# Cross-attention kernel on one core: weight loads dealt to other slots, other orders at head and end

## The chip, the cores and the metric

The kernel runs on one core of one Trainium2 chip. The metric is the device time of an execution in microseconds; a time is the median over several executions. Profiles come from one further execution, taken with the hardware profiler.

The engines are named as in the profile: PE does matmuls, PEld loads their stationary operand, DVE, ACT and POOL work elementwise, SP issues DMAs. "L694" is line 694 of the kernel.

## The reference

For 8 batches with 256 rows of 1024 values each, and a context of 256 rows per batch:

```
xn     = layernorm(x) * gamma + beta            # per row
Q      = xn @ Wq.T                              # 1024 x 1024, 32 heads of 32
scores = Q_h @ ctx_h.T / sqrt(32), masked       # context is keys and values
attn   = softmax(scores) @ ctx_h
out    = x + attn @ Wout.T
```

All is float32, and the mask is all true in these inputs.

## The kernel before

**Slots.** A slot n stands for batch `n // 8` and a group of four heads `n % 8`; there are N = 64. Loop pass n (L903) issues, for every engine, work of several slots: the scores of slot n+1, the values (probabilities times context) of slot n-2, a part of the query product of a later batch and a part of the output product of the batch before. The order in which each engine gets its instructions is the order in which the Python calls stand (`manual_schedule`, L115): nothing is reordered. SP, too, issues its DMAs in this order, and one that has to wait holds all those behind it.

**Softmax of a slot** (`softmax_parts`, L491). DVE adds the mask and finds the minimum (L515), ACT takes the exponential (L519), DVE inverts the sum (L526), POOL scales (L528), DVE transposes blocks of 32 (L534) into `pT`. A `tail` (L595) ends it: two DMAs pT<-pT (L600), the loads of a list `between`, then two DMAs pT<-pc (L604), which wait until the first two have landed. The loads of a list `ahead` are issued before the tail (L606). In slots 1 to 7 and near the end, the tail itself is put off into the next slot's softmax.

**Two products by Strassen's scheme.** For batches 3 to 7 the query product is done in seven steps, one a slot, from slot n = 8(b-1)+2 on (`firsts`, L782; `query_product`, L432; `Q_PRODUCTS`, L409). Each multiplies a quarter of x, or a sum of quarters, by a quarter of the weights, or a sum of them. Four of the weight operands stay in SBUF. The other three share one tile, `ring` (2 halves of 512 KB): T1 is used in slot n (product S1), B11 in slot n+2 (A11), T3 in slot n+4 (S3). They were written to DRAM once (`keep_wq`) and are loaded anew for every batch (`load_ring`, L405), in the slots that a table gives (L845). A load into a half must wait until the product before it has read that half; the product waits for each half by itself.

The output product of each batch goes the same way, seven products of four steps (`PRODUCTS`, L647; `STEPS`, L654), from 8 slots later on. Its weights `wo` (L162) hold B11, B21, B12 and B22, of which each is loaded by two DMAs of 512 KB (`load_wo`, L169), and four sums T1 to T4 that POOL makes (`sum_wo`, L177). The first batch's steps begin in slot 9: B11 first, then B21. In batch b's first slots the residual rows are loaded (`load_res`, L148); `store` (L734) adds the product to one of them on DVE and sends it out.

**Head** (L851 to L880). The first rows of x are normalised, transposed by PE into a bank, and copied out with gamma and beta in eight chunks `copy_x0` by ACT and DVE; PE takes the chunks in the same order for the first query (`first_q`, L279).

**End** (L1021 on). The last batch's output product is written out by hand. Its sums S2, S1 and S4 are made chunk by chunk (`end_sum`, L748), a chunk for each slot of the last four, and `end_steps` (L758) issues the matmuls; `last` holds the product A11, and four banks collect the rest. Chunk 1 is slot 61, whose values are copied out by ACT at L635.

Of the kernel before, what the change touches and what calls it, by code (L numbers as in the profile page):

```python
# [59 lines left out]
def xattn_kernel(  # L60
# [11 lines left out]
    nc = tc.nc  # L72
# [4 lines left out]
    NQ = NC  # L77
# [9 lines left out]
    N = B * NQ  # L87
# [75 lines left out]
    B11, B21, B22, T1, T2, T3, T4 = range(7)  # L163
    B12 = T1
# [105 lines left out]
    def copy_x0(s, c, engine):  # L270

        to, pt = xnT0[:, c, ts(s, P)], px0[s, c // (NC // 2)][:, c % (NC // 2), :]
        g, b = gam[:, c : c + 1], bet[:, c : c + 1]
        if engine is nc.scalar:
            nc.scalar.activation(to, pt, AF.Identity, bias=b, scale=g)
        else:
            nc.vector.tensor_scalar(to, pt, g, b, ALU.mult, ALU.add)
# [390 lines left out]
    def sum_at(b, name, c=slice(0, NK)):  # L668
        if name == "S2" and c.start == 0:
            s2s[b] = up.tile([P, NK, P], F32, tag="s2", name=f"s2_{b}")  # L670
        one, two, op = {
            "S3": ("A11", "A21", ALU.subtract), "S2": ("A22", "S3", ALU.subtract),
            "S1": ("S2", "A11", ALU.add), "S4": ("A12", "S2", ALU.subtract),
        }[name]
        nc.gpsimd.tensor_tensor(
            operand(b, name)[:, c], operand(b, one)[:, c], operand(b, two)[:, c], op
        )
# [70 lines left out]
    def end_sum(chunks, engine):  # L748
        for name, one, two, op in (
            ("S2", "A22", "S3", ALU.subtract), ("S1", "S2", "A11", ALU.add),  # L750
            ("S4", "A12", "S2", ALU.subtract),
        ):
            engine.tensor_tensor(
                end_operand(name)[:, chunks], end_operand(one)[:, chunks],
                end_operand(two)[:, chunks], op,
            )

    def end_steps(po, name, which, chunks, begins=(), cols=slice(0, 512)):  # L758

        for c in chunks:  # L760
            nc.tensor.matmul(  # L761
                po, end_operand(name)[:, c], wo[:, which, c, cols],
                start=c in begins, stop=True, skip_group_check=True,
            )
# [77 lines left out]
    ):  # L842
        away[n].append(partial(keep_wq, name, half))
    for n, b in firsts.items():
        for slots, name in (((n - 3, n - 2), "T1"), ((n, n), "B11"), ((n + 2, n + 2), "T3")):  # L845
            if b > SPLIT or name != "T1":
                for half, slot in enumerate(slots):
                    rings[slot].append(partial(load_ring, name, half))
# [4 lines left out]
    ln_norm(0, 0, nc.vector)  # L853
    ln_stats(0, 1, (1, 2))
    transpose_x0(0)
    early, late = (0, 1, 2, 3, 6, 7), (4, 5)
    for c in early + late:
        copy_x0(0, c, nc.vector if c > 5 else nc.scalar)
    nc.gpsimd.tensor_copy(xnT0[:, :, S], bet)
    ln_norm(0, 1, nc.vector)  # L860
    first_q(0, early + late)
# [41 lines left out]
    for n in range(N):  # L903
        b, i = divmod(n - NQ, NQ)
        new_q = new_qs[n]
        between = []
        if n % 2 and n + 1 < N:
            between.append(partial(load_v, n + 1))
        elif n % 2 == 0 and n + 4 < N:
            between.append(partial(load_k, n + 4))  # L910
        ahead = rings[n]
        if n + 3 in firsts or n + 2 in firsts:
            between, ahead = between + ahead, []
        if b >= 0:
            if b == B - 2 and i - 1 in (5, 6):
                between.append(partial(send, b, *ENDS_TO[i - 1]))
            if i < 4:
                between.append(partial(load_res, b, *((0, 0), (0, 1), (1, 1), (1, 0))[i]))
        between += [partial(load_x, *args) for args in loads[n]]
        between += [partial(load_mask, one) for one in masks[n]]  # L920
        if n < NQ:
            which, pair = (
                (B12, 0), (B22, 0), (B11, 0), (B12, 1), (B22, 1), (B11, 1), (B21, 0), (B21, 1)
            )[n]
            between.append(partial(load_wo, which, pair))
        if n == N - 4:
            again = xp.tile([P, NS, D], F32, tag="x", name="x_again")
            for s in range(NS):
                between.append(partial(nc.sync.dma_start, again[:, s, :], x[B - 1, ts(s, P), :]))

        if n + 1 < N:
            scores(n + 1)
        project_steps(n, 0)
        hooks, now, behind = {}, [], []
        for what, one, *args in evacuations[n]:
            if one == B - 2:
                now.append(partial(what, one, *args))
            else:
                place = "p1" if what is keep_p1 else "soon" if i == 2 else 0 if i in (3, 4, 6) else 1
                hooks.setdefault(place, []).append(partial(what, one, *args))  # L940
        if n >= 2:
            values(n - 2)
        project_steps(n, 1)
        copies = [partial(copy_q, q) for q in new_q]
        if n in halves and n % 2 == 0:
            make_q(halves[n], second=True, chunks=range(NC // 2, NC))
            copies.insert(0, partial(copy_q, halves[n]))
        for q in new_q:
            make_q(q)
        if n in products:  # L950
            query_product(*products[n])
            copies.append(partial(copy_product, *products[n]))
        for one in now:
            one()
        fill = []
        if n < 2:
            transpose_x1(2 * n)
            transpose_x1(2 * n + 1)
            fill = [partial(copy_x1, 2 * n), partial(copy_x1, 2 * n + 1)]
        elif n <= NQ:  # L960
            fill = [partial(ln_stats, *args, parts=(i,)) for args in stats[n] for i in range(3)]
            fill += [partial(blocks_x, *args) for args in trans[n]]
        if n + 1 < N:
            softmax(n + 1, copies, ahead, between, hooks, fill)
        else:
            copy_at(n - 2)
            for load in between:
                load()
        if b >= 0 and i == 1:
            sum_at(b, "S2", *((slice(NK - 1, NK),) if b == B - 2 else ()))  # L970
        later = []
        if n > NQ:
            for args in stats[n]:
                ln_stats(*args, later=later)
        for args in norms[n]:
            ln_norm(*args, nc.scalar)
        if n > NQ:
            for args in trans[n]:
                blocks_x(*args)
        for args in moves[n]:  # L980
            move_x(*args)
        for one in away[n]:
            one()
        for one in biases[n]:
            mask_bias(one)
        project_steps(n, 2)
        for one, slot in S3_SLOTS:
            if n == slot:
                sum_at(one, "S3")
        if b >= 0:  # L990
            for name in {2: ("S4",), 3 if b == B - 2 else 5: ("S1",)}.get(i, ()):
                sum_at(b, name)
            if i == 0 and b == B - 2:
                sum_at(b, "S2", slice(0, NK - 1))
        for slot, name in ((n + 2, "S1"), (n + 2, "S2"), (n + 1, "S4"), (n - 1, "S3")):
            if slot in firsts:
                sum_x(firsts[slot], name)
        if b == B - 2:
            if i > 2:
                add_kept(b, i, *ENDS_TO[i])  # L1000
        elif b >= 0 and i in (3, 4, 5):
            add_p1(b, *{3: (0, 1), 4: (1, 1), 5: (1, 0)}[i])
        for one in later:
            one()
        if n in halves and n % 2:
            make_q(halves[n], second=True, chunks=range(NC // 2))
        if n == 0:
            nc.gpsimd.tensor_scalar(gs, gam, NEG_SCALE, 1.0, ALU.mult, ALU.mult)
        if n < NQ:
            fold(n)  # L1010
        for one in sums[n]:
            one()
        if N - NQ + 2 < n < N - 1:

            c = n - (N - NQ + 3)
            if c == 0:
                last = ps_q.tile([P, 512], F32, tag="pq", name="po_last")
            end_steps(last, "A11", B11, (c,), (0,))
# [11 lines left out]
        )  # L1030

    nc.scalar.copy(end_p1, last)
    end_sum(slice(0, 2), nc.gpsimd)
    nc.gpsimd.tensor_tensor(r00, r00, end_p1, ALU.add)
    nc.gpsimd.tensor_tensor(r01, r01, end_p1, ALU.add)
    to_c11, to_c21, to_c22, to_c12 = (
        ps_s.tile([P, 512], F32, tag="sc", name=f"po_end_{i}") for i in range(4)
    )
    for c in range(2):
        end_steps(to_c11, "A12", B21, (c,), (0,))  # L1040
        end_steps(to_c21, "A22", T4, (c,), (0,))
    values(N - 2)
    copy_at(N - 2)
    end_sum(slice(2, 3), nc.gpsimd)
# [6 lines left out]
    copy_at(N - 1)  # L1051
    end_sum(slice(3, 4), nc.vector)
    first_cols, last_cols = slice(0, 384), slice(384, 512)
    end_steps(to_c22, "S1", T1, range(2), (0,))
    end_steps(s2t2, "S2", T2, (2,))
    for r in (r01, r10, r11):
        end_add(r, s2t2)
# [61 lines left out]
```

## Time and profile before

| | us |
|---|---|
| median of 3 runs | 575.49 |
| lowest and highest | 574.64, 575.76 |
| the profiled execution's own time | 579.34 |
| its span on the core | 577.6 |

| the profiled execution | us | share of the span |
|---|---|---|
| PE | 567.7 | 98% |
| PEld | 392.2 | 68% |
| DVE | 458.6 | 79% |
| ACT | 412.1 | 71% |
| POOL | 404.7 | 70% |

| stretch of the span, us | PE busy | DMA engines' busy share | GB/s |
|---|---|---|---|
| 0 to 8 | 6.43 | 0.75 | 241 |
| 8 to 150 | 139.16 of 142 | 0.72 | 219 |
| 150 to 240 | 90.00 of 90 | 0.77 | 228 |
| 240 to 250 | 7.81 of 10 | 0.65 | 196 |
| 250 to 545 | 295.00 of 295 | 0.69 | 199 |
| 545 to 578 | 29.31 of 33 | 0.37 | 115 |

The first table sets the profiled execution beside the plain runs. The second gives the time in which each engine worked, as a share of the span. The third cuts the span into stretches: the time in which PE was busy in each, and the mean share of the 16 DMA engines' time that was in use. The ends of matmuls are modelled, so a busy PE isn't PE at its peak; a gap in it is idle time.

### The profile page before, as it was taken

What the parts mean: (1) busy time and instruction counts of PE and PEld (TensorE: products, weight loads), DVE (VectorE), ACT (ScalarE), POOL (GpSimd) and SP (SyncE); (2) the same over time, 40 slices, a digit from 0 to 9 for tenths busy, and PEclk for the clock granted to TensorE, in tenths of its full rate; (3) what the DMA queues carried; (4) which work ended last, traced back from release to release, by engine and by line L of the source; (5) the groups of instructions that cost most, each with busy time, mean ns of one, the idle gap of its engine ahead of it and who ended that gap; (6) DMA issues with size and microseconds to landing.
All of it is one profiled execution on the core that took longest, in us unless ns stands there. A gap on an engine that the chain in (4) does not pass through costs nothing.

```text
span 577.6 us, 20001 instructions
## 1 busy us (share of the span) xinstructions
PE 567.7 (98%) x7162; PEld 392.2 (68%) x7162; DVE 458.6 (79%) x1695; ACT 412.1 (71%) x1425; POOL 404.7 (70%) x672
## 2 busy tenths in 40 slices
PE   8999998999999999899999999999999999999998
PEld 8788884666667777477776677667766777755444
DVE  6897887687878878678888888888877868879823
ACT  4688886677758857678577976779767866869820
POOL 1788998699896896665657775676656667448780
PEclk9999999999999999999999999999999999999999
DMA  8675778756778667776686767887658865436741
GB/s 312 224 211 184 218 240 209 244 172 196 196 229 271 215 188 219 225 222 202 181 247 181 233 196 201 237 257 217 186 160 254 239 192 147 130 112 182 214 154 74
DMA packets 47475, 117.98 MB, mean 204 GB/s; under 512 B 9104, under 2 KB 9872, under 8 KB 47376
## 3 DMA queue, kind: packets, MB, share of 16 engines
q1 hardware_dynamic: 47088, 116.69, 68.2%
q8 instruction: 57, 0.93, 0.7%
q14 instruction: 42, 0.34, 0.2%
q10 hardware_dynamic: 288, 0.01, 0.0%
HBM read 65.28 MB, written 11.53 MB: 133 GB/s over the span
## 4 chain that ended last, share of the span: by engine, by line
PE 79%; POOL 8%; DVE 6%; issue 2%; DMA 2%; ACT 1%; SPq 0%; DVEq 0%; POOLq 0%; ACTq 0%
PE po_S L694 17%; PE pq_A L440 16%; PE sc L479 10%; PE po_A L694 10%; PE pv L622 9%; PE pq_S L440 6%; POOL e L528 6%; PE pq L340 6%; DVE e L515 3%; PE po_end L761 2%; DVE pT L534 1%; PE po_last L761 1%; POOL wo L183 1%; DMA pT<-pT 1%; ACT e L519 1%
## 5 line engine op out<-in xcount | busy, mean ns | idle before, releaser
L528 POOL TENSOR_SCALAR e<-e,rden 128x256 f32<-128x256 f32 x512 | 237.0, 483 | 131.1 <-DVE rden L526 129.6
L519 ACT ACTIVATE e<-e,mn 128x256 f32<-128x256 f32 x512 | 254.0, 500 | 53.8 <-DVE mn L515 53.8
L534 DVE STREAM_TRANSPOSE pT<-e 128x512 f32<-128x512 f32 x256 | 180.7, 707 | 54.8 <-POOL e L528 43.8
L515 DVE CUSTOM_DVE_ANT_0 e<-sc,mb 128x256 f32<-128x256 f32 x512 | 185.9, 416 | 23.7 <-PE sc L479 23.2
L540 ACT COPY pc<-pT 128x512 f32<-128x512 f32 x128 | 79.0, 617 | 72.0 <-DVE pT L534 43.0
L519 ACT ACTIVATION_READ_ACCUMULATOR e<-e,mn 128x1 f32 x512 | 97.7, 191 | 0.0
L340 PE MATMUL pq<-xnT,wq 128*128 128x256 f32 (+1 forms) x368 | 84.1, 383 | 0.0
L340 PEld LDWEIGHTS pq<-xnT,wq 128*128 128x128 f32 x368 | 68.7, 190 | 14.3 <-issue 3.9
L479 PEld LDWEIGHTS sc<-k,qa 32*128 32x128 f32 x1024 | 46.2, 184 | 42.4 <-issue 20.6
L694 PE MATMUL po_S<-wo,at 128*128 128x512 f32 x152 | 74.5, 607 | 0.3 <-DVE r L736 0.3
L622 PE MATMUL pv<-pT,v 64*32 64x128 f32 x4096 | 74.3, 274 | 0.0
L622 PEld LDWEIGHTS pv<-pT,v 64*32 64x32 f32 x4096 | 56.9, 105 | 25.3 <-issue 11.9
L479 PE MATMUL sc<-k,qa 32*128 32x256 f32 x1024 | 73.6, 400 | 0.1
L694 PE MATMUL po_A<-wo,at 128*128 128x512 f32 x128 | 61.9, 616 | 4.2 <-issue 2.2
L694 PE MATMUL po_S<-wo,s 128*128 128x512 f32 x104 | 50.2, 606 | 0.3 <-DVE r L736 0.3
L515 DVE DVE_READ_ACCUMULATOR2_ANT mn<- 128x1 f32 x512 | 42.6, 83 | 0.0
L694 PEld LDWEIGHTS po_A<-wo,at 128*128 128x128 f32 x128 | 22.6, 190 | 29.2 <-issue 23.4
L526 DVE RECIPROCAL rden<-den 128x2 f32<-128x2 f32 x256 | 37.5, 146 | 5.9 <-ACT e L519 4.6
L440 PEld LDWEIGHTS pq_A<-xnT,wq 128*128 128x128 f32 x320 | 37.3, 192 | 4.8 <-issue 4.1
L694 PEld LDWEIGHTS po_S<-wo,at 128*128 128x128 f32 x152 | 25.6, 190 | 20.8 <-issue 19.3
L440 PE MATMUL pq_A<-xnT,wq 128*128 128x128 f32 x320 | 37.3, 275 | 0.0
L635 ACT COPY at<-pv 128x128 f32<-128x128 f32 x128 | 26.2, 253 | 8.7 <-PE pv L622 8.7
(95 smaller groups left out, 605.3 us busy)
## 6 DMA issues: line engine op xcount, KB each, us to landing
v<-in_kv_dram SPq DMA_DIRECT2D x32, 512.0 KB, 4.2
pT<-pT SPq DMA_DIRECT2D x128, 128.0 KB, 2.9
pT<-pc SPq DMA_DIRECT2D x128, 128.0 KB, 4.7
ring<-kept_T SPq DMA_DIRECT2D x18, 512.0 KB, 5.8
k<-in_kv_dram SPq DMA_DIRECT2D x32, 256.0 KB, 3.0
x<-in_x_dram SPq DMA_DIRECT2D x14, 512.0 KB, 5.5
r<-in_x_dram SPq DMA_DIRECT2D x28, 256.0 KB, 4.5
out_dram<-r SPq DMA_DIRECT2D x28, 256.0 KB, 3.9
```

The lines of the kernel that those rows point to most:

```text
L340: nc.tensor.matmul(pqs[n], wq[:, o, c, :], xnTs[b](c), start=(c == 0), stop=(c == NC - 1),)
L440: nc.tensor.matmul(pqs[b][:, o, :], w[:, c], x_[:, c], start=begins and o + c == 0, stop=c == NK - 1, skip_group_check=True,)
L479: nc.tensor.matmul(scs[n][j][:, s, :], qa[r, n % NQ, ts(s, P)], ks[n - n % 2][r, n % 2, :], start=True, stop=True,)
L515: nc.vector.tensor_tensor_reduce(out=e[:, s, :], in0=pss[j][:, s, :], in1=mbs[n // NQ], scale=1.0, scalar=NO_SCORE, op0=ALU.add, op1=ALU.m ...
L519: nc.scalar.activation(e[:, s, :], e[:, s, :], AF.Exp, bias=mn[:, s : s + 1], scale=-1.0, accum_out=den[:, s : s + 1],)
L526: nc.vector.reciprocal(rden, dens[j])
L528: nc.gpsimd.tensor_scalar(es[j][:, s, :], es[j][:, s, :], rden[:, s : s + 1], 1.0, ALU.mult, ALU.mult,)
L534: nc.vector.transpose(pT[:, :, :, j, :, :].rearrange("p a i s k -> p (a i) s k"), es[j].rearrange("p s (b t) -> p b s t", t=K),)
L540: nc.scalar.copy(pc[:, :, ts(j, 2)], pT[:, 1, :, ts(j, 2)])
L622: nc.tensor.matmul(pvs[n][r][j * HD : (j + 1) * HD], vs[n - n % 2][ts(r, 2 * K), i, ds(n % 2 * P + j * HD, HD)], pT[ts(r, 2 * K), :, i, j, ...
L635: nc.scalar.copy(ats[b, k][:, c, :, ts(r, 2), :], pv.rearrange("p a s k -> p s a k"))
L694: nc.tensor.matmul(po, operand(b, name)[:, c], wo[:, which, c], start=begins and c == 0, stop=c == NK - 1, skip_group_check=not begins,)
```

## The change

Five things are different.

- The six halves of the ring's operands are loaded in the six slots n-2 to n+3, one in each: T1 in n-2 and n-1 (before: n-3, n-2), B11 in n and n+1 (before: both in n), T3 in n+2 and n+3 (before: both in n+2). In slot n-2 the load stands between the two pairs of pT moves, in the others ahead of them.
- The eight loads of output weights go into slots 0 to 5, slots 2 and 4 taking two (before: one each in slots 0 to 7), in the same order.
- The first load of residual rows goes from slot 8 to slot 6.
- At the head, DVE copies chunks 5, 6 and 7 and ACT the other five (before: DVE 6 and 7), and the order for PE is 0, 1, 5, 2, 6, 3, 7, 4 (before: 0, 1, 2, 3, 6, 7, 4, 5).
- At the end, the sums of chunk 0 are made on POOL in slot 62, behind S3's sum and ahead of the additions of the batch before (before: with chunk 1, after the loop), and the first step of S1 is issued before the steps of chunk 1 (before: after the values of the last slot).

```diff
@@ ring's slots
-        for slots, name in (((n - 3, n - 2), "T1"), ((n, n), "B11"), ((n + 2, n + 2), "T3")):
+        for slots, name in (((n - 2, n - 1), "T1"), ((n, n + 1), "B11"), ((n + 2, n + 3), "T3")):
@@ head
-    early, late = (0, 1, 2, 3, 6, 7), (4, 5)
+    early, late = (0, 1, 5, 2, 6, 3), (7, 4)
     for c in early + late:
-        copy_x0(0, c, nc.vector if c > 5 else nc.scalar)
+        copy_x0(0, c, nc.vector if c > 4 else nc.scalar)
@@ loop
-        if n + 3 in firsts or n + 2 in firsts:
+        if n + 2 in firsts:
             between, ahead = between + ahead, []
...
-            if i < 4:
+            if i < 4 and b + i > 0:
                 between.append(partial(load_res, b, *((0, 0), (0, 1), (1, 1), (1, 0))[i]))
...
-        if n < NQ:
-            which, pair = (
-                (B12, 0), (B22, 0), (B11, 0), (B12, 1), (B22, 1), (B11, 1), (B21, 0), (B21, 1)
-            )[n]
+        for which, pair in {
+            0: ((B12, 0),), 1: ((B22, 0),), 2: ((B11, 0), (B12, 1)), 3: ((B22, 1),),
+            4: ((B11, 1), (B21, 0)), 5: ((B21, 1),),
+        }.get(n, ()):
             between.append(partial(load_wo, which, pair))
+        if n == NQ - 2:
+            between.append(partial(load_res, 0, 0, 0))
...
                 sum_at(one, "S3")
+        if n == N - 2:
+            end_sum(slice(0, 1), nc.gpsimd)
@@ end
-    end_sum(slice(0, 2), nc.gpsimd)
+    end_sum(slice(1, 2), nc.gpsimd)
...
-    for c in range(2):
-        end_steps(to_c11, "A12", B21, (c,), (0,))
-        end_steps(to_c21, "A22", T4, (c,), (0,))
+    end_steps(to_c11, "A12", B21, (0,), (0,))
+    end_steps(to_c21, "A22", T4, (0,), (0,))
+    end_steps(to_c22, "S1", T1, (0,), (0,))
+    end_steps(to_c11, "A12", B21, (1,))
+    end_steps(to_c21, "A22", T4, (1,))
     values(N - 2)
...
-    end_steps(to_c22, "S1", T1, range(2), (0,))
+    end_steps(to_c22, "S1", T1, (1,))
     end_steps(s2t2, "S2", T2, (2,))
```

## The prediction

> **What bounds the kernel now.** I read the busy line and the chain of waits first, then the waits of the whole run, then the timeline at each place that the diff touches.
>
> ```profile
> PE 567.7 (98%) x7162; PEld 392.2 (68%) x7162; DVE 458.6 (79%) x1695; ACT 412.1 (71%) x1425; POOL 404.7 (70%) x672
> ...
> PE 79%; POOL 8%; DVE 6%; issue 2%; DMA 2%; ACT 1%; SPq 0%; DVEq 0%; POOLq 0%; ACTq 0%
> ```
>
> PE (TensorE) carries the end: 79% of the chain. A matmul's end is modelled, so I count by starts: each form has a fixed pitch (0.43 us for 128x512, 0.216 us for the queries' 128x256), and what lies between two starts beyond it is lost. By that count PE loses almost nothing from 150 to 545 us, one place apart. Moving a DMA there gains nothing by itself; it can only add a wait. The gains must lie in these few places:
>
> ```profile
> DVE r L736 <- DMA r<-in_x_dram: 3.6, 1, 3.6
> PE po_A L694 <- issue: 2.2, 1, 2.2
> PE po_A L694 <- DMA wo<-in_woT_dram: 1.7, 1, 1.7
> ```
>
> The timeline round 98 us shows the first and third of them (start, duration, engine and line, and in brackets the idle time before it and who ended it):
>
> ```profile
> 85.89 0.71 SPq L173 DMA_DIRECT2D wo<-in_woT_dram  x1
> ...
> 98.06 1.13 PE L694 MATMUL po_A<-wo,at 128*128 128x512 f32 x2 [1.71 <-DMA wo<-in_woT_dram]
> ...
> 100.48 0.44 SPq L150 DMA_DIRECT2D r<-in_x_dram  x1
> ...
> 105.31 0.69 DVE L736 TENSOR_TENSOR r<-po_A,r 128x512 f32<-128x512 f32 x1 [3.57 <-DMA r<-in_x_dram]
> ...
> 106.15 1.95 PE L694 MATMUL po_S<-wo,s 128*128 128x512 f32 x4 [0.29 <-DVE r L736]
> ```
>
> The last piece of output weights is issued at 85.89, lands at 98.02 (12.1 us; the page's median for these is 7.2) and holds PE. The first residual, issued at 100.48, then holds DVE, and behind it in DVE's order stand the next scores' reductions: ACT and POOL go idle (POOL 4.05 us), and PE waits for the bank that DVE was to empty.
>
> The second of the waits is larger than its line:
>
> ```profile
> 243.75 1.87 PE L694 MATMUL po_A<-wo,at 128*128 128x512 f32 x2 [2.19 <-issue]
> ```
>
> From the values of slot 26 (starting 240.48) to the step after product S1 (249.95) pass 9.47 us; in slots 34 and 42 the same stretch takes 5.71. So 3.75 us are lost. The trace's packets say why: PE's instructions come in blocks of 16,384 bytes on queue q8 (57 of them), and this block moved at 241.28, 424 PE instructions after the one before it, instead of about 256, just when the DMA engines' busy share fell from 0.94 (229 to 240 us) to 0.38.
>
> [...]
>
> **The change part by part.**
>
> *Head, copies (L856 to L861).* ACT makes copies 0 to 3, 4, 5 from 7.62 to 9.83, six at 0.37; DVE makes 6 and 7 from 8.05 to 8.78. PE takes them in order and ends the first query on chunk 5. Afterwards ACT makes five, the last ready at 9.46, DVE three, the last at 9.14, and PE's order follows readiness. The query ends 0.37 earlier. DVE's normalisation of the second half starts 0.36 later and ends at 9.86; PE's transposes, at 10.29 before, can start at about 9.93. What follows to 15 us hangs on PE. The first matmul of the second query at 13.79 needs weights that landed before 14.67, the next block's time; I can't see its own landing, so the gain is between 0 and 0.37: I take **0.35**.
>
> *Output weights in slots 0 to 5, first residual in slot 6.* Eight 512 KB loads stay eight. The last is issued near 72.8 instead of 85.89; even at 12.1 us it lands by 85, with 13 us to spare before 98.06. The loss by starts is 98.06 - 95.76 - 0.43 = **1.87**. The residual goes past two slots of SP's queue; DVE's 3.57 us go, and PE's loss before 106.15 (last start 105.48, pitch 0.216) is **0.46**. What is late next? Values of slot 10 start at 100.19 and their pT landed at 98.4, 1.8 us of slack, less than the 1.87 + 0.35. But its own exchange crept behind those same weights (pT<-pT issued at 83.50, pT<-pc only at 91.76), so it comes earlier too. POOL and DVE form the chain from 106 to 149.76, where PE loses another **0.46** to the bank of L736 (149.09 + 0.216 to 149.76). They start about 4 us earlier, PE 2.7, so I count that loss as gone. Slots 2 and 4 carry one load more between the two pT moves: SP 0.44 us each, DMA about 1.7 us (512 KB at some 300 GB/s, from 0.97 busy at 314 GB/s in 35 to 46 us). pT_3 landed at 53.75 and is read at 59, slots 4's about 70 for 74: covered, with 2 us left at the tightest.
>
> *Ring by halves.* T1 moves from slots n-3, n-2 to n-2, n-1; B11's second half from n to n+1, T3's from n+2 to n+3, each now ahead of that slot's pT moves. PE waits for each half apart, so what counts is the second half: it is read 1.9 us after its product starts. T1: SP is free at 308.8 or 379.6, the load takes 3.7 to 4.1 us when alone (the two B11 loads at 248 and 250), against reads at 316.2 and 384.3: hidden. B11: free at 256, read at 266.8: hidden. T3 stands behind the four xnT moves: free at 207.5, 278.1, 348.5, 414.6 and 481.1 before, read at 210.2, 282.05, 350.2, 418.3 and 486.4. Those SP times were late themselves, because pT<-pT took 4 to 6.4 us behind 1 MB of T3; with half of it they come some 1.7 us earlier. With 3.9 us to land, slack is 0.5, 1.7, -0.5, 1.5, 3.1: a cost of **0.5** in all. Bounds: 0; with the page's median of 5.8 us, 1.4 + 0.2 + 2.4 + 0.4 = 4.4; without the earlier SP, 3.1 + 1.9 + 4.1 + 2.1 + 0.5 = 11.7. SP's 0.44 us ahead of a pT exchange is covered: values read it more than 8 us later.
>
> *End.* PE idles from about 551.5 until the copy of slot 61 lets step 1 start:
>
> ```profile
> 549.75 1.28 POOL L675 TENSOR_TENSOR at<-at 128x512 f32<-128x512 f32 x1
> ...
> 552.05 1.98 PE L761 MATMUL po_end<-wo,at 128*128 128x512 f32 x4 [0.36 <-ACT at L635]
> ```
>
> S1's chunk 0 is to fill that. But POOL is free for its sums only at 551.03 and two of them take about 1.0 (559.28 to 560.28 for the same shape): ready at 552.03. PE waits just as long, then does the 0.86 us there instead of at 561.5. POOL's later sums come 0.6 us later and are read 2 us after. **0**, between 0.1 lost and 0.5 gained.
>
> *Sum.* 0.35 + 1.87 + 0.46 + 0.46 - 0.5 = 2.64 us. The profiled execution took 579.34 us with a span of 577.6 (1.74 round it). Less its 3.75 us of fetching that is 575.59, against a median of 575.49: the unprofiled runs seem not to have that stall, and I don't count it as gain. So 575.49 - 2.64 = **572.85 us**.
>
> **The rivals.**
>
> *A. T3's second half is late (slower).* In the slots n+3 PE waits inside S3's product for a load that SP issues behind the moves. Gain 3.14 against 4.4 at the median latency: 576.75; against 11.7: 584. For it: margins of 0.5 to 1.7 us beside latencies that spread over 3.7 to 7.9. Against it: DMA is half idle there (shares round 0.5 at 345 to 350 us). It turns slower by more than 0.2% once the five waits sum to over 4.3 us.
>
> *B. Instruction blocks starve.* Loads spread evenly leave fewer dips of the DMA engines, and a block like that of 241.28 comes late in ordinary runs: 3.75 us each. Once: 572.85 + 3.75 = 576.6. Against: the bytes of the busiest two slots in a row, counted from the list of issues, grow little (4.3 MB from 4.0), and 1 MB of T3 and of B11 at once are gone.
>
> *C. Weights were not late without the profiler.* Then only the copies, part of the stores' 0.9 and the 0.5 remain: 575.49 - 0.6 = 574.9, no change that shows.
>
> *D. Evener DMA gains more:* small waits that the profile hides in its one execution, or a fetch stall that some plain runs had too: 571.
>
> **How the numbers follow.** A measurement of this kernel can tell about 0.2%, 1.15 us, from no change. Forecast 0.68, D 0.12, C 0.06, A 0.09 (0.06 of it slower, the rest same), B 0.05 (half same, half slower). A third of C still counts as faster. Faster 0.68 + 0.12 + 0.02 = 0.82; same 0.04 + 0.03 + 0.02 = 0.09; slower 0.06 + 0.03 = 0.09. The range reaches from D's 570.9 to 575.6, where C and the mild part of A lie; only the far ends of A and B are left out.
>
> **What would show it.** Right: no wait of PE on wo and none of DVE on r near 100 us; PE's transposes of the second half near 9.9 us; the store wait near 149 us gone; slot 18 beginning some 3 us earlier; the end from slot 62 on as long as before. Wrong: waits of S3's product on the ring's DMA, several q8 blocks over 400 instructions apart with "issue" idle on PE, or PE waiting on DVE or POOL between 106 and 150 us.

## The result, and the profile after

The changed kernel takes 579.19 us (median of 10 runs, 576.16 to 582.29) against 575.1 for the kernel before in the same session (10 runs, 573.86 to 576.42). The ratio is 1.0067 with a 95% interval of 1.0047 to 1.0088: 3.9 us slower (2.7 to 5.1), where 2.64 us faster was forecast. Its profiled execution took 579.02 us with a span of 577.2, nearly that of before (577.6). But before's span holds the stall of 3.75 us at slot 26, which the prediction set aside, and after's only 1.29 of it. A ratio leaves out executions more than 1.5% above the fastest of their kernel: three in all, of 582.1, 949.82 and 1989.13 us.

What the prediction called 3.75 us of fetching is two things. PE was idle for 2.19 of them. The rest, some 1.6, is the work behind, done at half clock: by the trace's clock record PE had half its clock from 243.67 to 247.09. Stretches of before with the granted clock of PE in the column PEclk:

```profile
core 0: us, PE busy (x) PEld busy (x) DVE busy (x) ACT busy (x) POOL busy (x), PEclk, DMA share, GB/s
241.00:245.00 4.00, 1.81 (x42) 1.11 (x27) 2.12 (x11) 2.40 (x10) 1.45 (x2) 0.83 0.53 111
245.00:246.00 1.00, 1.00 (x4) 0.59 (x3) 0.34 (x1) 0.00 (x0) 0.00 (x0) 0.50 0.93 373
```

The busy line and the chain's shares, from the page of the kernel after:

```profile
PE 566.8 (98%) x7162; PEld 392.1 (68%) x7162; DVE 459.2 (80%) x1696; ACT 411.8 (71%) x1424; POOL 403.8 (70%) x675
...
PE 85%; DMA 4%; POOL 3%; DVE 3%; ACT 2%; SPq 1%; issue 1%; DVEq 0%
```

The amount of work is the same. DMA's share of the chain is 4% instead of 2%. The waits of the whole run name what PE stands on (us in total, times, longest):

```profile
DVE st L226 <- DMA x<-in_x_dram: 6.7, 3, 3.4
...
PE po_A L694 <- ACT qa L349: 2.4, 1, 2.4
...
PE po_A L694 <- issue: 1.0, 1, 1.0
PE pq_S L440 <- DMA ring<-kept_T: 1.0, 1, 1.0
...
PE pq_A L440 <- DMA ring<-kept_T: 0.7, 1, 0.7
```

The waits on wo and on the residual that the prediction showed are both gone. Three new ones have come: PE behind ACT's qa, and S1 and S3 behind the ring.

Comparing the start of every slot's values in the two traces gives the places where the difference between the kernels changes (plus: after loses; times of the kernel before):

| stretch | us | what it is |
|---|---|---|
| to 44 us | +0.45 | PE's first transpose is 0.42 later, since x landed later in this execution; the copies win 0.25, and 0.29 is lost to ACT's copies at 36 us |
| 74 to 93 us | +0.37, +2.26 | the values at 74.54 wait for their pT; PE waits for ACT's qa at 92.57 |
| 93 to 153 us | -1.98, -0.53, -0.28, -0.56 | the waits on wo, on the residual and on the store's bank are gone |
| 241 to 253 us | -2.46 | the stall at slot 26, 1.29 instead of 3.75 |
| 347 to 365 us | +1.01, +0.09 | S3 of batch 5 waits for T3's second half |
| 449 to 457 us | +1.24 | S1 of batch 7 waits for T1's second half |
| 549 us to the end | +0.93, -0.95 | S1's first step is done here, not after the last values |

So between these two traces the forecast gains are there: 1.98 for 1.87, and 0.53 and 0.56 for 0.46 each. A new loss of 2.6 us stands just ahead of them and takes most of it back, and the ring costs another 2.25.

**The new loss near 92 us.** First the kernel before, its timeline from 70 to 87 us:

```profile
70.07 2.07 SPq L600 DMA_DIRECT2D pT<-pT  x2
...
73.57 1.15 SPq L604 DMA_DIRECT2D pT<-pc  x2
74.77 3.76 SPq L327 DMA_DIRECT2D xnT<-xe  x6
78.63 1.93 SPq L600 DMA_DIRECT2D pT<-pT  x2
...
81.23 0.44 SPq L130 DMA_DIRECT2D x<-in_x_dram  x1
...
85.86 0.69 DVE L226 BATCH_NORM_STATS2 st<-x 128x6 f32<-128x512 f32 x1
```

SP issues batch 3's first x at 81.23. It landed at 85.83, and DVE began its statistics at 85.86. No wait is shown, and none can be seen by looking for waits: the slack was 0.03 us. Now the same stretch of after:

```profile
71.92 2.66 SPq L600 DMA_DIRECT2D pT<-pT  x2
...
77.18 1.15 SPq L604 DMA_DIRECT2D pT<-pc  x2
78.38 4.10 SPq L327 DMA_DIRECT2D xnT<-xe  x6
82.58 1.16 SPq L600 DMA_DIRECT2D pT<-pT  x2
...
84.42 0.44 SPq L130 DMA_DIRECT2D x<-in_x_dram  x1
...
88.93 0.69 DVE L226 BATCH_NORM_STATS2 st<-x 128x6 f32<-128x512 f32 x1 [2.79 <-DMA x<-in_x_dram]
91.52 0.62 ACT L540 COPY pc<-pT 128x512 f32<-128x512 f32 x1 [3.61 <-DVE rden L526]
92.05 0.83 ACT L349 ACTIVATE qa<-pq,qa 128x256 f32<-128x256 f32 x2
92.57 3.70 PE L694 MATMUL po_A<-wo,at 128*128 128x512 f32 x8 [2.39 <-ACT qa L349]
```

With two 512 KB loads in slot 4, the next pT<-pT starts 1.85 us later and pT<-pc, which waits for its landing, 3.61 later. SP issues in order, so the six xnT moves and then x of batch 3 come late too (84.42). DVE stands on x for 2.79 us, with the current softmax's transposes behind it; ACT's copy of them, then its qa, then PE follow. That is the 2.26.

The 0.37 ahead of it is slot 4's own exchange. Its second pT<-pc, issued at 67.80 behind the two loads, landed at 74.85, 7.04 us later, when the values that read it had begun. Before, then after:

```profile
74.09 1.16 PE L622 MATMUL pv<-pT,v 64*32 64x128 f32 x64
```

```profile
74.54 1.53 PE L622 MATMUL pv<-pT,v 64*32 64x128 f32 x64
```

**The ring.** After, timeline round slots 37 and 49:

```profile
340.73 2.43 SPq L327 DMA_DIRECT2D xnT<-xe  x4
343.20 0.58 SPq L407 DMA_DIRECT2D ring<-kept_T  x1
...
348.34 1.38 PE L440 MATMUL pq_A<-sx,ring 128*128 128x128 f32 x10 [0.75 <-DMA ring<-kept_T]
...
443.38 0.57 SPq L407 DMA_DIRECT2D ring<-kept_T  x1
...
451.87 1.38 PE L440 MATMUL pq_S<-sx,ring 128*128 128x128 f32 x10 [0.97 <-DMA ring<-kept_T]
```

T3's second half leaves SP at 343.20, behind four xnT moves, and lands at 348.29. T1's leaves at 443.38, 5.6 us before S1 starts on the first half (448.95), and lands only at 451.83, 8.45 us after its issue.

### The profile page after: what moved, and what is told of

Read it like the earlier page. It is cut to its first block, busy times and chain, and to the rows that moved or that the text cites. A ratio compares the mean times of both kernels' runs of the same rounds, so it can differ in the third digit from the quotient of the medians.

```text
span 577.2 us, 20009 instructions
## 1 busy us (share of the span) xinstructions
PE 566.8 (98%) x7162; PEld 392.1 (68%) x7162; DVE 459.2 (80%) x1696; ACT 411.8 (71%) x1424; POOL 403.8 (70%) x675
## 4 chain that ended last, share of the span: by engine, by line
PE 85%; DMA 4%; POOL 3%; DVE 3%; ACT 2%; SPq 1%; issue 1%; DVEq 0%
PE po_S L694 19%; PE pq_A L440 15%; PE pv L622 11%; PE sc L479 10%; PE pq L340 10%; PE po_A L694 9%; PE pq_S L440 6%; PE po_end L761 2%; DMA ring<-kept_T 2%; POOL e L528 2%; DVE e L515 1%; PE po_last L761 1%; ACT e L519 1%; DMA x<-in_x_dram 1%; DMA pT<-pc 1%
```

## The experiments

Ratios are to the kernel before, measured in the same session. The theory is that two things cost: x of batch 3 late behind slot 4's double load, and the ring's second halves late. The rivals differ by experiment.

**The parts alone.** The ring's table and its two lists only:

```diff
-((n - 3, n - 2), "T1"), ((n, n), "B11"), ((n + 2, n + 2), "T3")
+((n - 2, n - 1), "T1"), ((n, n + 1), "B11"), ((n + 2, n + 3), "T3")
-        if n + 3 in firsts or n + 2 in firsts:
+        if n + 2 in firsts:
```

> The kernel before with only the ring's loads moved (T1 to n-2, n-1; B11 to n, n+1; T3 to n+2, n+3). Theory: the ring holds the loss. Second halves of T1 and T3 land late, and late instruction blocks on PE recur, so 2.3 to 4.5 us are lost against before, and its runs scatter over several us as those of the whole change do. Rival: the ring is hidden and the loss comes from the head; then within 0.6 us of before.

Measured: 578.37 us, 1.005 (1.0027 to 1.0073), some 2.9 us slower (1.6 to 4.2). Its trace has S3 waiting twice, for batches 5 and 6, 1.7 us of PE's time. Of the late instruction blocks that were also expected nothing shows: the stall at slot 26 is 0.2 us there.

The output weights in slots 0 to 5 with the residual in slot 6, the ring as before:

> The kernel before with only the output weights in slots 0 to 5 and the first residual in slot 6. Theory: the double load of slot 4 holds SP back by about 4 us, x of batch 3 comes late, and PE loses 2.8 us at slot 9, which eats the 3.3 us won at the waits on wo and r: between -0.7 and +0.3 us. Rival that the head holds the loss: +2 to +4 us. The forecast's own sum would be -2.8.

Measured: 576.74 us, 1.0032 (1.001 to 1.0054), 1.8 slower (0.6 to 3.1), more than the theory allowed. In its trace PE waits in front of slot 9 for 2.00 us (0.24 before), and then gains 2.14, 0.53, 0.28 and 0.56, as after does. It shows one thing more. The line of that wait, and then busy times by stretch with PE's clock:

```profile
91.41 5.34 PE L694 MATMUL po_A<-wo,at 128*128 128x512 f32 x8 [2.00 <-ACT qa L349]
```

```profile
core 0: us, PE busy (x) PEld busy (x) DVE busy (x) ACT busy (x) POOL busy (x), PEclk, DMA share, GB/s
84.00:92.00 8.00, 6.00 (x38) 4.70 (x37) 5.86 (x22) 5.13 (x20) 5.50 (x11) 0.96 0.98 296
92.00:93.00 1.00, 1.00 (x2) 0.34 (x1) 1.00 (x6) 0.82 (x2) 1.00 (x1) 0.50 0.82 291
93.00:96.00 3.00, 3.00 (x6) 1.25 (x5) 2.03 (x14) 2.76 (x12) 3.00 (x4) 0.71 0.53 129
```

PE runs at half clock for about 3.4 us (0.04 of 8, half of 1 and 0.29 of 3 us are missing, 1.7 in all, and twice that is the time at half): the 8 matmuls that take 3.70 us before and after take 5.34. One such stretch lowers the mean clock of an execution to 0.997 (half of 3.4 us in 575). Of this kernel's 19 executions 8 have at least 0.999 and a median of 575.00 us, 7 have 0.997 and 577.03, and 4 have 0.994 and 580.71. So in about half of them the wait seems to cost its own length and about as much again. By the clock records of the traces, the stretches at half clock between 50 and 550 us lasted 3.41 us (five, in executions with a mean clock of 0.997) or 6.83 (one, at 0.994). The length of the idle time doesn't tell whether one comes: in this trace one begins by the end of 2.00 us of idle time, and in after's trace, whose mean clock is 1.000, 2.39 us have none behind them.

Copies and the end only, and the residual in slot 6 only:

> The kernel before with only the two new orders, copies at the head and steps at the end. Theory: the copies win 0.2 to 0.35 us, the end nothing, since S1's first step waits for POOL as long as PE waited for ACT before: -0.4 to 0 us. Rival: the end costs 0.5 us or more through POOL's later sums.

> The kernel before with only the first residual loaded in slot 6 instead of 8. Theory: DVE's wait of 3.6 us goes, and with it PE's 0.46 near 106 us and 0.46 near 149 us, while 256 KB more in slot 6 make the late weights a little later: 0 to -0.9 us. Rival: the load delays the weights that PE waits for at 98 us by its own 0.9 us, and nothing is won: 0 to +0.9.

Measured: 576.25, 1.0005 (0.9987 to 1.0023), no change; and 576.45, 1.0015 (0.9991 to 1.0038). The residual alone goes ahead of the last output weights on SP's queue, and in its trace PE waits longer for these. Timeline of the kernel with the residual alone:

```profile
99.53 2.08 PE L694 MATMUL po_A<-wo,at 128*128 128x512 f32 x2 [2.99 <-DMA wo<-in_woT_dram]
```

The wait on wo, 1.71 in before's trace, is 2.99. In 7 of its 14 executions the mean clock is under 0.9985, against 4 of 57 of the kernel before; its trace has both, the wait of 2.99 us and a mean clock of 0.994.

The head's two groups of transposes start 3.47 us apart before and 3.22 after: the copies give 0.25 (forecast 0.35). But it isn't kept. In the traces of all four kernels that have the new copies and end, and in none of the others, PE loses 0.29 us more near 36 us, and by 44 us the copies' gain is used up. ACT's copies of batch 1's x (L305) end later there; why, and whether PE's loss hangs on that alone, stays open.

**Which half of the ring.** T1 alone in n-2 and n-1, and T3's second half alone in n+3:

> Of the ring, only T1 moved (slots n-2 and n-1 instead of n-3 and n-2); B11 and T3 as before. Theory: T1's second half, issued a slot before its use behind whatever DMA has queued, is late in some batches by 1 us and more[...]: +1 to +2 us, about half of the ring's 2.9. Rival: T3 carries nearly all: then within 0.6 us of before.

> Of the ring, only T3 split (second half in slot n+3, behind the xnT moves); T1 and B11 as before. Theory: one to three of the five batches wait 0.8 to 1 us for it: +1 to +2.5 us. Rival: T1 carries nearly all: within 0.6 us.

Measured: T1 576.03, 1.0017 (1.0003 to 1.003), 1.0 slower; T3 577.82, 1.0039 (1.0021 to 1.0057), 2.2 slower. Together 3.2, for the ring's 2.9: B11's split costs nothing that shows. Timeline of T1 alone, then of T3 alone:

```profile
373.29 0.57 SPq L407 DMA_DIRECT2D ring<-kept_T  x1
...
381.71 2.05 PE L440 MATMUL pq_S<-sx,ring 128*128 128x128 f32 x16 [0.95 <-DMA ring<-kept_T]
```

```profile
337.16 2.44 SPq L327 DMA_DIRECT2D xnT<-xe  x4
339.64 0.58 SPq L407 DMA_DIRECT2D ring<-kept_T  x1
...
344.80 2.05 PE L440 MATMUL pq_A<-sx,ring 128*128 128x128 f32 x16 [0.72 <-DMA ring<-kept_T]
```

The trace of T3 alone shows something else that matters: it has no wait of PE on wo, and none of PE on the residual. Between 93 and 153 us it wins the same 1.98, 0.53, 0.28 and 0.56 over before's trace, though nothing was changed there. These waits differ from execution to execution. In ten traces of kernels with the output weights and the first residual in their old slots, PE's idle time on wo is between 0 and 2.08 us, with a median of 0.76; before's 1.71 is the third largest. From the waits of the ring's trace:

```profile
PE po_A L694 <- DMA wo<-in_woT_dram: 0.2, 1, 0.2
```

**Is it slot 4's second load?** The weights' part again, with that load in slot 3:

```diff
-            0: ((B12, 0),), 1: ((B22, 0),), 2: ((B11, 0), (B12, 1)), 3: ((B22, 1),),
-            4: ((B11, 1), (B21, 0)), 5: ((B21, 1),),
+            0: ((B12, 0),), 1: ((B22, 0),), 2: ((B11, 0), (B12, 1)), 3: ((B22, 1), (B11, 1)),
+            4: ((B21, 0),), 5: ((B21, 1),),
```

> Output weights and residual as in the run with weights alone, one load moved: the second load of slot 4 stands in slot 3. Theory: slot 4's double load is what held SP back, so x of batch 3 comes as early as before, PE's wait of 2 to 3 us at slot 9 goes and the waits on wo and r stay away: -1.5 to -3 us against before. Rival: slot 3's tail passes the same delay on: as the run with weights alone, +1.

Measured: 576.04, 1.0023 (1.0005 to 1.0042), 1.3 slower, as the rival had it: slot 4 in itself isn't the culprit. Timeline of this kernel:

```profile
70.03 1.52 PE L622 MATMUL pv<-pT,v 64*32 64x128 f32 x64 [2.82 <-ACT e L519]
70.89 1.15 SPq L604 DMA_DIRECT2D pT<-pc  x2
```

The delay only comes a slot earlier. The 2.82 us are a wait for the exchange itself: the two pT<-pc of slot 3, issued from 60.26 on behind the two loads, landed only at 69.94 and 70.33, after the work of ACT that the line names. The next pT<-pc goes out at 70.89 (65.84 before), and DVE stands on x again, so that PE waits for another 2.55 us at 97.31. A second load in either slot delays what SP issues after it.

**The stall at slot 26.** Batch 4's T1 isn't loaded; this kernel leaves it out, and its product S1 uses what the ring holds:

```diff
-            if b > SPLIT or name != "T1":
+            if b > SPLIT + 1 or name != "T1":
```

> The kernel before without the two loads of T1 for batch 4 (1 MB round slots 23 and 24; product S1 of batch 4 then works on stale weights, so this part of the output is left wrong). Theory: [...]the stall at slot 26 (0.9 to 3.7 us in four of five traces) goes and the next blocks there stay under 330 instructions apart: -0.8 to -1.5 us in the median and fewer long executions. Rival: the stall has to do with PE's own pace, not DMA: no change, and a block over 400 instructions apart stands there again.

Measured: 575.51, 0.9999 (0.9986 to 1.0011), not the 0.8 to 1.5 faster that the theory expected. Its trace lacks the stall (the stretch is 3.76 us shorter). But so do the traces of the residual alone and of the load in slot 3, where T1 is loaded as before, so the load isn't shown to be the cause. In thirteen other traces the stretch loses 0.2 to 2 us; before's 3.75 is the largest. A trace without it and a median like that of before: to set it aside when summing was right.

That a late block of instructions is the cause was the prediction's reading of one trace, and it isn't settled. In the four traces where PE is idle for over 1 us there without a named cause, the idle time ends 1.3 to 1.6 us after such a block has moved (before: 16,384 bytes on queue q8 from 241.28 to 242.38, PE at work again at 243.75), which fits. But before's trace has blocks as far apart, 431 and 422 instructions (at 47.41 and 381.35), with no idle time of PE.

**The late x, tested by itself.** Batch 3's statistics go one slot later, so that DVE doesn't stand on x; once in the kernel before, as a control, once with the weights' part, and once with everything but the ring:

```diff
-                stats=(first - 10, first - 9) if b == SPLIT else (first - 11, first - 9),
+                stats=(first - 9, first - 8) if b == SPLIT else (first - 11, first - 9),
```

> The kernel before, with only the statistics of batch 3's two x tiles moved one slot later (from slots 8 and 9 to 9 and 10); DVE no longer stands behind the x load of slot 6, nothing else moves. A control. In the trace of before that load landed 0.03 us ahead of DVE, so nothing waited there: the theory (after's loss near 90 us is DVE waiting for this x) expects no change, 575.5 within 0.6, and the waits on wo near 98 us as they are. Rival (the slot in which DVE does these statistics matters by itself, since 1.4 us of DVE's work per tile now falls into slots 9 and 10, where DVE also makes the stores): slower by 0.5 to 1.5.

> The output weights in slots 0 to 5 and the residual in slot 6 (which alone gave about 1.8 us slower), and batch 3's statistics one slot later as in the control. Theory (the weights did what was forecast, but the doubled slot 4 made x of batch 3 late by 3 us, DVE stood on it with the exchange behind it, and PE idled 2.4 us[...]): DVE has no wait on x, PE no wait of over 1 us between 84 and 96 us, nearly no run with a granted clock under 0.9985, and the gain forecast appears, 1.9 to 2.8 less than before: about 572.9. Rival (the exchange's own DMAs stand behind the doubled weights and the six moves, so ACT's copies stay late without any x): PE still loses about 2 us near 92 us, and the time stays 1 to 2 slower than before.

> The whole change without the ring part (copies, weights, residual, end), and batch 3's statistics one slot later. Theory: the run before it, and 0 to 0.4 less for the head's copies: about 572.6, the fastest of all. Rival (as in the run before it): 1 to 2 slower than before.

Measured: the control 576.46, 1.0018 (1.0004 to 1.0032), 1.0 slower, as its rival had it; the weights' part 573.42, 0.997 (0.9958 to 0.9983); all but the ring 573.44, 0.9975 (0.996 to 0.9989). One line turns the weights' part from 1.8 slower into 1.7 faster (1.0 to 2.4), and from 11 of 19 executions with a lower clock to 1 of 22. Timeline of the weights' part with late statistics:

```profile
83.50 0.45 SPq L130 DMA_DIRECT2D x<-in_x_dram  x1
...
89.36 3.70 PE L694 MATMUL po_A<-wo,at 128*128 128x512 f32 x8
...
97.65 1.25 DVE L226 BATCH_NORM_STATS2 st<-x 128x6 f32<-128x512 f32 x2
```

That x is still issued 2.3 us later than before, but DVE comes to it only at 97.65, and PE's matmuls start at 89.36 with no wait. The rival (the exchange itself stays late, and PE with it) falls. Nor is the line a gain of its own: alone it makes the kernel slower. In this trace PE waits once more, 1.53 us for an xnT move at 101.67; the trace of all but the ring has no such wait.

For the control's trace the same kernel was run once more:

> The control with batch 3's statistics one slot later once more, for its trace. Theory: the waits on wo (about 1.9 us of PE's time) and on the residual stay as in before, and the 1 us that it was slower is found in slots 9 and 10, where DVE's statistics now stand ahead of or behind the store's addition. Rival: the wo wait itself is longer[...].

It took 577.03 us in its one run. Timeline:

```profile
111.13 1.24 DVE L226 BATCH_NORM_STATS2 st<-x 128x6 f32<-128x512 f32 x2
...
115.53 0.69 DVE L732 TENSOR_TENSOR r<-po_S,r 128x512 f32<-128x512 f32 x1
116.28 0.30 PEld L694 LDWEIGHTS po_S<-wo,at 128*128 128x128 f32 x2 [1.12 <-DVE r L732]
```

The waits on wo and on the residual are as before (1.98 and 0.42 of PE's time), and a new one of 0.88 has come at 116.28, where the second x's statistics stand ahead of the store in DVE's order. That fits the 1.0, from one trace. The traces with the weights' part and late statistics don't have this new wait, so the control isn't a clean one. Against it the weights' part is worth about 2.8 us, of which some 0.9 is the control's own wait; against the kernel before, 1.7 (1.0 to 2.4), where the prediction summed 2.79.

**The ring's queue, tested by itself.** T3's second half in n+3 as in the experiment above, with the moves of later batches' xnT one slot later, and those moves alone as control; and T1 with both halves in slot n-2:

```diff
-                moves=tuple(first - 6 + (i + 2) // 6 for i in range(16)),
+                moves=tuple(first - 5 + (i + 2) // 6 for i in range(16)),
```

> Only T3 split over slots n+2 and n+3 (which alone gave about 2.2 us slower), and the 16 moves of every later batch's normalised x one slot later, so that no xnT move stands on SP's queue ahead of T3's second half. Theory (the cost is S3 waiting for a second half that SP issues late, behind the moves of slot n+2): that half is issued 3 to 4 us earlier against its use, no wait of S3 on the ring, and the time is that of the moves alone, within 0.5. Rival (the cost is the load's place in the crowd of transfers in slot n+3, not the queue): still 1.5 to 2.5 slower than the moves alone.

> Control: the kernel before with only those moves one slot later. Both theories: within 0.6 of before (575.3), or slower by up to 2 if the last moves now land late for the queries of slot first.

> Only T1, both halves in slot n-2 and each ahead of the exchange's moves (n-2 and n-1 gave about 1.0 slower, with S1 waiting 1.12 and 0.92 for the second half in its trace). Theory (the second half of slot n-1 is late): it is now issued 8 us earlier, no wait of S1, and the time is before's, within 0.5. Rival (it is T1 standing ahead of the exchange's moves that costs): 1 slower or more, with values waiting for pT.

Measured: T3 with the moves 579.61 (6 runs), 1.0081 (1.005 to 1.0112); the moves alone 582.1 (6 runs), 1.0119 (1.0087 to 1.0151); T1 with both halves early 575.28, 0.9996 (0.9974 to 1.0017). Timeline of T3 with the moves:

```profile
342.79 0.53 SPq L407 DMA_DIRECT2D ring<-kept_T  x1
...
347.24 2.94 PE L440 MATMUL pq_A<-sx,ring 128*128 128x128 f32 x24
```

S3 no longer waits for the ring. Beside its control the split costs nothing, it is 2.5 us faster. But the control failed as a control: the moves alone cost 6.8 us, in waits of po_S behind DVE's store L736 (0.9 to 1.9 us in the slots of S1). Why, I haven't settled, nor why the split eases it. So the queue as the cause of T3's cost stays argued. For T1 it is clearer: with the second half a slot earlier S1 doesn't wait in the trace, and the loss no longer shows in the time (0.2 faster, between 1.5 faster and 1.0 slower). Both halves stand between the two pairs of pT moves there, not ahead of them as the expectation has it, so its rival (T1 ahead of the exchange costs) wasn't tested by the time alone. Timeline of that kernel:

```profile
371.90 0.92 SPq L407 DMA_DIRECT2D ring<-kept_T  x2
...
379.05 3.73 PE L440 MATMUL pq_S<-sx,ring 128*128 128x128 f32 x32
```

**Is that all?** The whole change, with the statistics one slot later:

> The whole change as it is, with only batch 3's statistics one slot later. Theory (the two causes are all there is): what the weights lost comes back, and the ring's cost of about 2.9 (1.6 to 4.2) stays on top of the whole without the ring (573.44, 1.4 faster than before): 1.5 slower than before, between 0.2 and 2.8, so about 576.7; no wait of PE at 90 to 93 us, waits on the ring's second halves as before. Rival (the parts meet: the ring's cost is larger or smaller beside the new weights): 3 or more slower, or no slower than before.

Measured: 574.94 us (22 runs), 1.0 (0.9985 to 1.0015). So the one line takes back what the change had lost, 3.9 us. The expected 1.5 slower lies outside the interval (0.9 faster to 0.9 slower). Beside all but the ring (1.4 faster than before) the ring costs about 1.4 here, against 2.9 alone; the intervals overlap, so a smaller cost isn't shown. The two traces, 571.2 and 572.5, differ by one wait of S3 (1.23) and 0.15:

```profile
344.74 2.05 PE L440 MATMUL pq_A<-sx,ring 128*128 128x128 f32 x16 [0.97 <-DMA ring<-kept_T]
```

The fastest kernels are the two with the late statistics and the ring of before, at 573.4 us: 1.4 to 1.7 us faster than before, and some 5.5 faster than the change.

## Why the prediction was wrong

- **The step that failed.** The extra load of slots 2 and 4 was called "covered, with 2 us left at the tightest", and so put at 0. It measured 2.6 us in after's trace. The exchange of slot 4, put at "about 70 for 74", landed at 74.85 and cost 0.37. The other 2.26 lie behind it on SP's queue, where the step didn't look: the xnT moves and x of batch 3, whose slack against DVE was 0.03 us. In plain runs, taking DVE's reading of x out of the way gives back 3.9 us, more than the trace's 2.6; part of it is the clock, which was under 0.9985 in 4 of after's 10 executions and in 1 of 22 with the one line.
- **wo and residual, 1.87 + 0.46 + 0.46:** the waits were there and the change removes them (1.98, 0.53, 0.56 in after's trace). Their sizes were read from one execution in which they were large, and in plain runs the part is worth 1.7 us (1.0 to 2.4), not 2.79. That the two traces agree so closely is luck.
- **Head copies, 0.35:** 0.25 came, and was lost again at 36 us; the step "What follows to 15 us hangs on PE" didn't look that far. Too small for the medians.
- **The ring, -0.5:** mis-sized. Alone it cost 2.9 (1.6 to 4.2), within the whole about 1.4. For T3 the slacks named the right place: batch 5, at -0.5, lost 1.01. For T1 "SP is free at 308.8 or 379.6, the load takes 3.7 to 4.1 us when alone" took the latency of a lone load. In slot n-1 it is not alone: for batch 7 k, T1's first half, a residual and pT<-pc are issued in the 2.8 us before, the DMA engines are 0.98 busy from 444 to 448 us, and it took 8.45 us. For batches 5 and 6, whose times the prediction gives, it took 6.98 and 6.31 and landed in time all the same (313.06 and 381.58); batch 7, the late one, was not worked out.
- **End, 0:** right.
- **Fetch stall, not counted:** right; without it the median was the same. Its size was read as fetching alone, though almost half of it was PE's half clock (1.6 of 3.75 us); that the rest is fetching isn't shown.
- **Rivals.** A was right in kind (S3 waits behind the moves), but the waits in after's trace sum to 1.0 on T3, not 4.3 or more; by itself it wouldn't have made the change slower. B: no; the stall in slot 26 is 1.29 in after's trace and nearly absent in the ring's. C: in part; a gain of the weights comes out in plain runs once x is out of DVE's way, but smaller than read from before's trace. D: no. The deciding mechanism was in none of them.
- **What stays open.** After's trace, less the stall at slot 26, is 2.1 us longer than before's (577.2 - 1.29 against 577.6 - 3.75), the plain runs 3.9. The lower clock explains part: 4 of after's 10 executions show it, with a median of 581.14 against 577.71 for the others. Another part may be that before's trace lost more than usual between 93 and 153 us. The rest can't be apportioned from one trace of each.

## What to carry to other kernels

Before adding a load to a DMA queue that issues in order (here SP's: x of batch 3 went out at 84.42 us instead of 81.23), follow every DMA issued behind it to its reader, not only those that the load was placed among, and list the slack of each: a landing 0.03 us ahead of its reader shows no wait and is the first to break. A load's latency is to be taken from the slot that it moves into, with all that is issued there (8.45 us for a half of T1, not 3.7 to 4.1). Where a new wait stands just ahead of the one removed, moving its reader (here two statistics, one slot later) can be worth more than moving the load. And the size of a wait is better read from several executions than from one: the wait on wo was anything from 0 to 2.08 us in ten traces.

## What the runs showed of the hardware

- In six traces an idle time of PE of 1.90 to 2.99 us had a stretch at half clock beside it, which lasted 3.41 us in five of them (mean clock 0.997) and 6.83 in one (0.994). In one of the five, that of the weights' part, 8 matmuls took 5.34 us instead of 3.70.
- The length of the idle time alone didn't decide it. Idle times of 1.90 us (the moves alone), 2.00 (the weights' part), 2.08 (copies and end), 2.19 (before), 2.82 (the load in slot 3) and 2.99 (the residual alone) have such a stretch beside them; 1.98 (T1 alone), 2.39 (after) and 2.55 (the load in slot 3, a second time) don't. Of the weights' part 11 of 19 executions show a mean clock of 0.997 or less.
- A 512 KB load of a ring's half took 3.75 and 4.10 us where SP issued the other half and nothing else between 246.8 and 252.3 us (B11 of batch 4, before's trace), and 6.31 to 8.45 where k, another half, a residual and a pT<-pc had been issued just ahead (T1's second halves, after's trace).
